# An LSTM over 512 steps with its input projection by fast matrix multiplication: when the bias differences are made, how far ahead sums run, and when finished blocks of the head are stored

## The chip, the core and the metric

The kernel runs on one core of a Trainium2 chip. The core has a matmul engine (TensorE, PE in the profile), three engines for elementwise work (VectorE, DVE; ScalarE, ACT; GpSimd, POOL) and SyncE (SP), which issues all of this kernel's DMAs. Each engine takes its instructions in order, and they wait for one another by semaphores. The metric is the device time of one execution in microseconds (us).

## The reference

`x` has 32 rows of 512 steps with 512 features. An LSTM runs over the steps, started from `cond_1024`, and its outputs are added to `x`:

```python
xW = jnp.einsum('ntd,dg->ntg', x, Wx) + b          # 4*512 gate columns
def step(carry, xw_t):
    prev_h, prev_c = carry
    a = xw_t + prev_h @ Wh
    i, f, o = sigmoid of a's first three quarters
    g = jnp.tanh(a[:, 3 * Hd:])
    next_c = f * prev_c + i * g
    next_h = o * jnp.tanh(next_c)
    return ((next_h, next_c), next_h)
x = x + all next_h
```

All data are float32. The gate bias `b` is drawn with a spread of 0.1, so it is not zero.

## The kernel before

**A step.** Step t needs its row of xW in a PSUM bank. TensorE adds `h @ Wh` to it (`h_part`, L272: 16 matmuls of 128x512, which the profile counts as 32). Then `cell` runs: ScalarE's sigmoids and tanh (L285 to L290, from step 18 on L298 to L305), VectorE's products (L288, L289, L291; later L302 to L307) and a transpose that gives the next `h` (L292, later L309). The next `h_part` needs that `h`. TensorE fills the time in between with the projection `x @ Wx`.

**The projection, from step 19 on.** Steps 19 to 498 form 15 groups of 32 steps. A group's projection is done by a fast matrix multiplication in two levels. The outer level has 26 products ("slots"), each of a sum of x blocks (U, `U_SUMS`, `U_OF`; made on VectorE by `make_sum`, L504, in eight buffers, `free_u`) and a sum of weight blocks (V, `V_SUMS`, `V_OF`), where V is the same in all groups. The inner level does each slot by seven products of half size, `ROW` (L590). Four copies or adds bring a slot's result out of PSUM into one of some 16 buffers (`free_c`; `evacuate`, L656 to L672). Sums of results (W, `W_SUMS`, `W_OF`; `w_op`, L450, 128x1024 on VectorE) give 16 output blocks a group. A finished block is appended to `done_blocks`; `store_blocks` (L463) issues its DMA to DRAM (L467), gives its buffer back to `free_c` and counts it in `gr.stored`. `load_xw` (L723) brings the rows of a step back (L732), and ScalarE puts them into the step's bank (L743).

**The head, steps 0 to 18.** Their projection is done plainly, 32 matmuls of 256 columns a block and step (`plain_block`, L200), while VectorE makes the V sums (`v_sum`, L781 and L784, with `v_store`, L788, into DRAM `vdram`) and the x sums of group 0 (`pair_sum`, L535 to L541, of rows that `load_row`, L525, brings). V sums 8 to 25 live in ten rooms (`V_ROOMS`), which are parts of other buffers, so a room is written again only after the store of what stood in it. `load_v` (L703, L708) brings V rows back for the slots from number 4 on. The rows of steps 5 to 18 start from a copy of the bias into their bank: L960 for step 0's two plain blocks (14 and 15), L1074 for the following steps'. Finished rows of steps 14 to 18 are parked in DRAM (`kept`, L874, loaded again at L726).

**Bias differences.** In the groups, the bias enters through some of the slots' banks, which start from one of six rows: -b2, b0-b3, b3, b0-b1+b2, b1, b1-b0 (`BIAS_OF`, `seed_tile`; ScalarE copies them in, L633). `make_seeds` (L831) computes these rows from `seeds_at`, a tile of 64 partitions with the four bias rows, each as two halves of 4 elements a partition (also subtracting the first half from the second), and stores them in DRAM (L843). `load_seeds` (L845) loads them, spread over all partitions, from step 3 on.

**What sets the order.** The program is one list written out by a planner; every engine follows its part of the list. In the head, each step t emits `h_part`, the stores that wait, and then chunks (`HEAD_PLAINS` plain blocks, `HEAD_STREAM` quarters of products). A stream chunk of m quarters first calls `load_v_ahead`, `store_blocks` and `u_ahead(m)`, which makes every U sum that the next m quarters need, then `evacuate`. A chunk after the cell calls `row_jobs(4)`, `u_ahead(m + 24)` and then `w_op` as long as the planner's account `room["dve"]` allows; then come the matmuls. The cell of a step stands after its first chunk (from step 10 on, after its second). `room["dve"]` is an account in ns: matmuls add to it, every operation on VectorE takes its cost (`cost_dve`: 150 + 1.05 a column, 1225 for a W sum, 1091 for a U sum). `jobs` are the V sums and the like of the first steps, shared out over a step's chunks. From step `HEAD_STEPS` = 19 on, the loop sets the account to `3800 + min(0, room)` at each step and calls `w_op` while it is over 1000; it calls `store_blocks` after every `w_op`.

**SyncE's queue** issues DMAs in the order of the list. There are eight semaphores for them in turn, so each DMA waits until the one eight before it has landed, and a store that waits for VectorE holds up all that is behind it.

Of the kernel before, what the change touches and what calls it, by code (L numbers as in the profile page):

```python
# [7 lines left out]
F32 = mybir.dt.float32  # L8
# [97 lines left out]
def kernel(  # L106
# [59 lines left out]
    def load_x_ahead():  # L166
        nc.sync.dma_start(
            out=xnat[:, 2, 0 : HEAD - 2 * TC].rearrange("p t q b -> p (t q b)"), in_=x[2][:, 0 : (HEAD - 2 * TC) * P]
        )
# [253 lines left out]

    wait_to_store = [True]

    def w_op(short=False):
# [35 lines left out]

    def store_blocks():  # L463
        for gr, o, buf, src in done_blocks:
            mo, j = divmod(o, 4)
            tau = TAU.index(mo)
            nc.sync.dma_start(  # L467
                out=xwd[gr.g % 2][2 * tau : 2 * tau + 2, :, j].rearrange("m p c -> p m c"),
                in_=buf_of(buf).rearrange("p (m n) c -> p m (n c)", m=2),
            )  # L470
            if src is None:
                free_c.append(buf)
            else:
                release(gr, src)
            gr.stored[tau] += 1
        done_blocks.clear()

# [349 lines left out]

    seeds_at = work.tile([P // 2, 10, 2, 4], F32, name="seeds_at")
    by_part = lambda a: a.rearrange("j (h p k) -> p j h k", h=2, p=P // 2)

    def make_seeds():  # L831
        b = [seeds_at[:, i] for i in range(4)]
        neg2, d03, b3, all3, b1, d10 = (seeds_at[:, 4 + i] for i in range(6))
        for j in range(4):
            sub(seeds_at[:, j, 1], seeds_at[:, j, 1], seeds_at[:, j, 0])
        sub(d10, b[1], b[0])
        sub(neg2, b[1], b[2])
        sub(neg2, neg2, b[1])
        sub(d03, b[0], b[3])
        nc.scalar.copy(b3, b[3])  # L840
        nc.scalar.copy(b1, b[1])
        sub(all3, b[2], d10)
        nc.sync.dma_start(out=by_part(seed_dram), in_=seeds_at[:, 4:10])  # L843

# [31 lines left out]
    with tc.manual_schedule():  # L876
        nc.vector.memset(sring[0], 0.0)
        nc.vector.memset(tanh_c, 0.0)
        nc.scalar.activation(hbuf, tanh_c, AF.Sigmoid)
        load_x(0, 0, 5)  # L880
# [11 lines left out]
        for j in range(NJ):  # L892
            nc.sync.dma_start(
                out=bias_full[j * B : (j + 1) * B], in_=bias[j : j + 1].to_broadcast([B, W])
            )
        nc.sync.dma_start(out=seeds_at[:, 0:4], in_=by_part(bias))
        nc.sync.dma_start(out=h_init.rearrange("p q b -> p (q b)"), in_=h0)
# [6 lines left out]
        load_x(1, 0, 5)  # L904
        load_x_ahead()
        for n in range(4):
            for j in range(NJ):
                nc.tensor.matmul(
                    park_banks[n % 3][j * B : (j + 1) * B],
                    tanh_c[:, 0:B],  # L910
                    tanh_c.unsqueeze(1).to_broadcast([P, 4, P]),
                    start=True,
                    stop=True,
                )
# [15 lines left out]
        keep(FIRST)  # L930
        make_seeds()
        jobs = {}
        sums = lambda *ids: [lambda i=i: v_sum(i) for i in ids]
        jobs[0] = sums(13, 14, 15, 16)
        jobs[1] = sums(17, 18, 19, 20)
        jobs[2] = sums(21, 22, 23)
# [25 lines left out]
        for t in range(T):  # L962
# [4 lines left out]
            kept_stores.clear()  # L967
            store_blocks()
            c, rest = divmod(t + 6, TC)
# [25 lines left out]
            if t < HEAD_STEPS:  # L995
# [22 lines left out]
                for i, (kind, m, cs) in enumerate(chunks):  # L1018
# [16 lines left out]
                    else:  # L1035
                        load_v_ahead()
                        store_blocks()
                        u_ahead(m)
# [6 lines left out]
                        else:  # L1045
                            row_jobs(4)
                            u_ahead(m + 24)
                            while wqueue and (
# [35 lines left out]
            if t == HEAD_STEPS:  # L1084
                room["dve"] = max(room["dve"], -2600.0)
            wait_at_end[0] = t >= END - 2
# [86 lines left out]
```

## Time and profile before

| | us |
|---|---|
| median of 3 runs | 3084.79 (3084.72 to 3087.29) |
| profiled execution | 3085.83 |
| its span, first to last instruction | 3084.1 |
| TensorE busy, share of the span | 3061.4, 99% |
| VectorE busy | 2340.9, 76% |
| ScalarE busy | 1466.8, 48% |
| GpSimd busy | 243.0, 8% |
| mean granted TensorE clock | 0.999 |
| moved by DMA | 753.21 MB, mean 244 GB/s |

How to read the lines that follow. A timeline line has start and length in us, engine, line of the kernel, operation, output<-inputs, shapes, count, and in brackets how long the engine had been idle and what released it. SPq marks an issue on SyncE's queue, PEld the load of a matmul's stationary operand. A line of waits has engine, output and line, the instruction waited for, and then the sum in us, how often, and the longest. Where an instruction waited for several, the view names the one that came last by the profile, and this can be another engine than the one that truly held it up.

### The profile page before, as it was taken

To read this page: it belongs to the slowest core of one execution; us is meant where nothing else is said; L and a number is where in the kernel's file an instruction comes from. 1 tells how busy PE (TensorE), PEld (TensorE's weight loads), DVE (VectorE), ACT (ScalarE), POOL (GpSimd) and SP (SyncE) were. 2 spreads that over 40 slices of the span, in tenths; PEclk is the share of its full clock that TensorE was granted. 3 is DMA by queue.
4 is the path that set the end of the run, shared out by engine and by line. 5 is a ranking of instruction groups with operands and counts; after the bars stand their busy time and mean duration, and the time that the engine had idled before them with its cause. 6 is when DMAs were issued, how large, how long until landed. Compare 5 with 4: busy or idle time off the path is not lost.

```text
span 3084.1 us, 108287 instructions
## 1 busy us (share of the span) xinstructions
PE 3061.4 (99%) x43624; PEld 1658.8 (54%) x43624; DVE 2340.9 (76%) x6310; ACT 1466.8 (48%) x5476; POOL 243.0 (8%) x508
## 2 busy tenths in 40 slices
PE   9999999999999999999999999999999999999998
PEld 5755555555555555555555555555555555555675
DVE  7588787787877878778787887878778787787644
ACT  1344545445454544545444444454544545454444
POOL 0000000000000000000000000000000000000110
PEclk9999999999999999999999999999999999999999
DMA  9888878787787878878787787877878777788530
GB/s 319 272 288 279 272 246 262 241 259 243 252 260 243 259 243 257 256 231 274 232 268 243 242 272 234 271 239 243 267 241 260 242 247 263 245 264 270 162 91 18
DMA packets 320149, 753.21 MB, mean 244 GB/s; under 512 B 52128, under 2 KB 103968, under 8 KB 319136
## 3 DMA queue, kind: packets, MB, share of 16 engines
q1 hardware_dynamic: 319648, 746.28, 75.3%
q8 instruction: 344, 5.64, 0.8%
q14 instruction: 157, 1.29, 0.1%
HBM read 564.67 MB, written 184.56 MB: 243 GB/s over the span
## 4 chain that ended last, share of the span: by engine, by line
PE 97%; DVE 1%; DMA 1%; ACT 0%; issue 0%; SPq 0%; ACTq 0%; DVEq 0%
PE gbank L272 54%; PE xbank L590 32%; PE bbank L590 5%; PE xbank L272 3%; PE xbank L209 1%; PE gbank L200 1%; PE xbank L200 1%; DMA r<-in_L_cond_Wx_dram 0%; PE bbank L200 0%; DMA r<-in_x_grouped_dram 0%; DMA vring<-in_L_cond_Wx_dram 0%; DVE cbuf L450 0%; DVE vring L784 0%; DVE ubuf L784 0%; DVE xnat L450 0%
## 5 line engine op out<-in xcount | busy, mean ns | idle before, releaser
L272 PE MATMUL gbank<-wh_sb,ht 128*32 128x512 f32 (+1 forms) x16256 | 1775.3, 575 | 4.0 <-DVE ht L309 1.6
L272 PEld LDWEIGHTS gbank<-wh_sb,ht 128*32 128x32 f32 x16256 | 606.7, 110 | 825.9 <-issue 700.0
L590 PE MATMUL xbank<-vring,ubuf 128*32 128x256 f32 (+1 forms) x13584 | 852.4, 369 | 5.8 <-ACT cbuf L672 2.3
L298 ACT ACTIVATE s<-gbank 128x128 f32<-128x128 f32 x944 | 264.7, 281 | 1162.9 <-PE gbank L272 1162.3
L590 PEld LDWEIGHTS xbank<-vring,ubuf 128*32 128x32 f32 x13584 | 527.7, 110 | 298.4 <-issue 136.0
L302 DVE TENSOR_TENSOR prod<-s 128x128 f32<-128x128 f32 x988 | 283.6, 287 | 461.6 <-ACT s L299 457.0
L317 POOL TENSOR_TENSOR oc<-xnat,ht 128x128 f32<-128x128 f32 x504 | 242.8, 482 | 2803.1 <-DVE ht L309 1294.9
L305 ACT ACTIVATE tanh_c<-s 128x64 f32<-128x64 f32 x988 | 253.6, 257 | 234.6 <-DVE s L303 232.0
L309 DVE STREAM_TRANSPOSE ht<-hbuf 128x64 f32<-128x64 f32 x986 | 242.0, 245 | 72.5 <-DVE hbuf L307 0.9
L743 ACT COPY gbank<-xw 128x512 f32<-128x512 f32 x458 | 275.3, 601 | 2.7 <-DMA xw<-xwd 2.4
L303 DVE TENSOR_TENSOR s<-prod 128x64 f32<-128x64 f32 x988 | 222.2, 225 | 34.0
L307 DVE TENSOR_TENSOR hbuf<-o,tanh_c 128x64 f32<-128x64 f32 x988 | 204.6, 207 | 31.8 <-ACT tanh_c L305 31.2
L450 DVE TENSOR_TENSOR cbuf<-cbuf 128x1024 f32<-128x1024 f32 x178 | 216.6, 1223 | 1.0
L299 ACT ACTIVATE s<-gbank 128x64 f32<-128x64 f32 x944 | 217.0, 230 | 0.0
L590 PE MATMUL xbank<-vring,r 128*32 128x256 f32 (+1 forms) x3216 | 208.6, 357 | 0.0
L590 PE MATMUL xbank<-vring,xs 128*32 128x256 f32 (+1 forms) x3120 | 202.4, 356 | 0.0
L590 PE MATMUL bbank<-vring,ubuf 128*32 128x256 f32 (+1 forms) x2600 | 185.0, 342 | 0.0
L590 PEld LDWEIGHTS xbank<-vring,r 128*32 128x32 f32 x3216 | 123.4, 110 | 78.8 <-issue 46.0
L590 PEld LDWEIGHTS xbank<-vring,xs 128*32 128x32 f32 x3120 | 120.8, 110 | 57.8 <-issue 22.8
L300 ACT ACTIVATE o<-gbank 128x128 f32<-128x128 f32 (+1 forms) x493 | 148.7, 302 | 0.0
L656 ACT COPY cbuf<-xbank 128x512 f32<-128x512 f32 x228 | 132.7, 582 | 27.8 <-PE xbank L590 15.4
L590 PEld LDWEIGHTS bbank<-vring,ubuf 128*32 128x32 f32 x2600 | 101.2, 110 | 67.7 <-issue 38.6
(171 smaller groups left out, 2558.0 us busy)
## 6 DMA issues: line engine op xcount, KB each, us to landing
vring<-vdram SPq DMA_DIRECT2D x310, 896.0 KB, 6.2
xw<-xwd SPq DMA_DIRECT2D x1920, 64.0 KB, 4.6
xwd<-cbuf SPq DMA_DIRECT2D x142, 512.0 KB, 4.7
xwd<-r SPq DMA_DIRECT2D x79, 512.0 KB, 4.4
out_dram<-oc SPq DMA_DIRECT2D x255, 128.0 KB, 3.6
xnat<-in_x_dram SPq DMA_DIRECT2D x62, 512.0 KB, 5.4
xs<-in_x_grouped_dram SPq DMA_DIRECT2D x45, 512.0 KB, 4.7
vring<-vdram SPq DMA_DIRECT2D x33, 512.0 KB, 5.0
```

Source lines behind the costliest of these rows:

```text
L272: nc.tensor.matmul(dst[j * B : (j + 1) * B], state["ht"][:, k], m, start=False, stop=True, skip_group_check=True)
L298: nc.scalar.activation(s[:, u, 0:2], g[:, n_, 0:2], AF.Sigmoid)
L299: nc.scalar.activation(s[:, u, 2], g[:, n_, 3], AF.Tanh)
L302: nc.vector.tensor_mul(prod[:, u], s[:, u, 0:2], s[:, u, 2:4])
L303: add(nxt[:, u, 3], prod[:, u, 0], prod[:, u, 1])
L305: nc.scalar.activation(tanh_c[:, HALVES[u]], nxt[:, u, 3], AF.Tanh)
L307: nc.vector.tensor_mul(hbuf[:, HALVES[u]], o[:, u], tanh_c[:, HALVES[u]])
L309: nc.vector.transpose(ht[:, 2 * u : 2 * u + 2].rearrange("p q b -> p (q b)"), hbuf[:, HALVES[u]])
L317: (nc.gpsimd if t < T - 8 else nc.vector).tensor_add(oc[:, tt % 2], x_of(t), ht)
L450: op(c_of(dst), c_of(src), c_of(bb))
L590: nc.tensor.matmul(dst[j * B : (j + 1) * B, cols], left_of(gr, s, r)[:, j * B : (j + 1) * B], right_of(row, slot, RIGHT[r])[:, cols], star ...
L743: nc.scalar.copy(bank_of(t), src)
```

## The change

Four edits.

1. **Bias differences.** The four bias rows are loaded by four DMAs (one a row) after the head's x loads, in place of one DMA ahead of `h0` and `Wh`. They land where the results want them (b1 and b3 in their final place), -b2 is now zero minus b2 (its row is set to zero at the start), where it was b1 - b2 - b1, and three of the four half differences are one operation. `make_seeds` has six operations on VectorE and none on ScalarE, where it had nine and two, and is called between the V sums 19 and 20 of step 1; before, it was called ahead of step 0. Its store moves along.
2. **Stores.** In steps 0 to 14 `store_blocks` leaves the blocks that were finished since its last call for the next call, if more than three buffers are free.
3. **U sums.** In the last chunk of steps 7 to 16 the look-ahead is `m + 40` quarters in place of `m + 24`, if more than one U buffer is free.
4. **Step 19.** The planner's account is set to -2000 there; before, it was only raised to -2600 where it was below.

```diff
+    old = [0]
...
-    def store_blocks():
-        for gr, o, buf, src in done_blocks:
+    def store_blocks(keep_new=False):
+        fresh = done_blocks[old[0] :] if keep_new and len(free_c) > 3 else []
+        for gr, o, buf, src in done_blocks[: len(done_blocks) - len(fresh)]:
...
-        done_blocks.clear()
+        done_blocks[:] = fresh
+        old[0] = len(fresh)
...
-    seeds_at = work.tile([P // 2, 10, 2, 4], F32, name="seeds_at")
+    seeds_at = work.tile([P // 2, 8, 2, 4], F32, name="seeds_at")
...
+    BIAS_AT = (6, 4, 7, 2)
+
     def make_seeds():
-        b = [seeds_at[:, i] for i in range(4)]
-        neg2, d03, b3, all3, b1, d10 = (seeds_at[:, 4 + i] for i in range(6))
-        for j in range(4):
-            sub(seeds_at[:, j, 1], seeds_at[:, j, 1], seeds_at[:, j, 0])
-        sub(d10, b[1], b[0])
-        sub(neg2, b[1], b[2])
-        sub(neg2, neg2, b[1])
-        sub(d03, b[0], b[3])
-        nc.scalar.copy(b3, b[3])
-        nc.scalar.copy(b1, b[1])
-        sub(all3, b[2], d10)
-        nc.sync.dma_start(out=by_part(seed_dram), in_=seeds_at[:, 4:10])
+        neg2, d03, b3, all3, b1, d10, b0, b2 = (seeds_at[:, i] for i in range(8))
+        sub(seeds_at[:, 2:8:2, 1], seeds_at[:, 2:8:2, 1], seeds_at[:, 2:8:2, 0])
+        sub(b2[:, 1], b2[:, 1], b2[:, 0])
+        sub(d10, b1, b0)
+        sub(neg2, neg2, b2)
+        sub(d03, b0, b3)
+        sub(all3, b2, d10)
+        nc.sync.dma_start(out=by_part(seed_dram), in_=seeds_at[:, 0:6])
...
         nc.vector.memset(tanh_c, 0.0)
+        nc.vector.memset(seeds_at[:, 0], 0.0)
...
-        nc.sync.dma_start(out=seeds_at[:, 0:4], in_=by_part(bias))
         nc.sync.dma_start(out=h_init.rearrange("p q b -> p (q b)"), in_=h0)
...
         load_x_ahead()
+        for j in range(NJ):
+            nc.sync.dma_start(out=seeds_at[:, BIAS_AT[j] : BIAS_AT[j] + 1], in_=by_part(bias[j : j + 1]))
...
         keep(FIRST)
-        make_seeds()
...
-        jobs[1] = sums(17, 18, 19, 20)
+        jobs[1] = sums(17, 18, 19) + [make_seeds] + sums(20)
...
-            store_blocks()
+            store_blocks(t < HEAD - 4)
...
-                        store_blocks()
+                        store_blocks(t < HEAD - 4)
...
-                            u_ahead(m + 24)
+                            u_ahead(m + (40 if i == len(chunks) - 1 and 6 < t < HEAD_STEPS - 2 and len(free_u) > 1 else 24))
...
             if t == HEAD_STEPS:
-                room["dve"] = max(room["dve"], -2600.0)
+                room["dve"] = -2000.0
```

## The prediction, made before the changed kernel ran

> **What bounds the kernel now.** I read the page first, then TensorE's own waits, then the timeline of each engine in the first 310 us, then the DMA share in windows there.
>
> ```profile
> PE 3061.4 (99%) x43624; PEld 1658.8 (54%) x43624; DVE 2340.9 (76%) x6310; ACT 1466.8 (48%) x5476; POOL 243.0 (8%) x508
> PE 97%; DVE 1%; DMA 1%; ACT 0%; issue 0%; SPq 0%; ACTq 0%; DVEq 0%
> ```
>
> TensorE is busy for all but 22.7 us of the 3084.1 us span, and it is 97% of the chain that ended last. The change adds and removes no matmul, so all that it can win is TensorE's idle time, plus time at a lowered clock. TensorE's waits, longest first:
>
> ```profile
> PE xbank L200 <- ACT xbank L960: 4.1, 1, 4.1
> ...
> PE xbank L590 <- ACT cbuf L672: 2.3, 2, 1.5
> PE xbank L590 <- ACT xbank L633: 1.7, 1, 1.7
> ...
> PE gbank L272 <- DMA wh_sb<-in_L_cond_Wh_dram: 1.3, 1, 1.3
> PE gbank L272 <- DVE hbuf L307: 1.1, 1, 1.1
> PE xbank L590 <- ACT xnat L672: 0.9, 1, 0.9
> ```
>
> All of these stand in steps 0 to 19. Asked for 240 us onward, the same view holds the L307 wait alone (it begins at 239.0), until the last steps' waits for h at L309. What can be won therefore lies in the first 240 us.
>
> **The seeds (make_seeds and its loads).** The largest wait, on TensorE and on ScalarE:
>
> ```profile
> 31.89 1.06 PE L272 MATMUL gbank<-wh_sb,ht 128*32 128x512 f32 x8 [1.35 <-DMA wh_sb<-in_L_cond_Wh_dram]
> 37.07 6.11 PE L200 MATMUL xbank<-r,xnat 128*32 128x256 f32 x64 [4.11 <-ACT xbank L960]
> ```
>
> ```profile
> 36.24 0.20 ACT L840 COPY seeds_at<-seeds_at 64x8 f32<-64x8 f32 x1 [33.90 <-DVE seeds_at L835]
> ```
>
> ```profile
> 16.00:20.00 4.00, 4.00 (x82) 3.26 (x75) 1.68 (x3) 0.00 (x0) 0.00 (x0) 1.00 0.46 89
> 37.00:42.00 5.00, 4.93 (x48) 2.54 (x49) 3.45 (x7) 1.48 (x6) 1.08 (x1) 0.50 0.74 248
> 54.00:56.00 2.00, 2.00 (x44) 1.59 (x40) 2.00 (x4) 0.24 (x1) 0.00 (x0) 1.00 0.32 121
> ...
> 83.00:89.00 6.00, 6.00 (x87) 3.90 (x81) 5.18 (x8) 1.80 (x5) 1.21 (x1) 1.00 0.19 69
> 175.00:200.00 25.00, 23.27 (x340) 12.03 (x336) 18.42 (x34) 9.69 (x26) 1.67 (x2) 1.00 0.81 286
> ```
>
> (Windows: stretch, length, then busy us of PE, PEld, DVE, ACT, POOL, the granted clock, DMA share, GB/s.) The copy at L960 puts the bias under step 0's plain blocks. It needs only bias_full, but on ScalarE's in-order queue it stands behind L840, which waits 33.9 us for VectorE to reach make_seeds. The change takes both small copies off ScalarE, so L960 can run as soon as the bias is loaded, and the 4.11 us go. The stall also halved the granted clock (0.50 from 37 to 42 us): 4.93 us of work at half speed is 2.46 us lost. The gap of 1.7 us in step 13 leaves the clock at 1.00 (175 to 200), so this goes too.
>
> SyncE's queue there:
>
> ```profile
> 11.26 0.64 SPq L896 DMA_DIRECT2D seeds_at<-in_L_cond_b_dram  x1
> 14.65 0.35 SPq L897 DMA_DIRECT2D ht<-in_cond_dram  x1
> 18.34 2.05 SPq L899 DMA_DIRECT2D wh_sb<-in_L_cond_Wh_dram  x4
> ```
>
> These issues come one by one, each when an earlier transfer has landed (eight semaphores in rotation). Without L896 the h0 load takes its turn at 11.26 and the first wh row the turn at 14.65, 3.7 us sooner, into a stretch where the DMA share is 0.46 (0.54 x 4 = 2.2 us unused). wh is what TensorE awaits for 1.35 us at 31.89. Bounds 0 and 1.35; I take 1.35, since 2.2 us exceed it. The four bias loads now stand behind the x loads, and behind them on SyncE the first V stores, whose rooms are not written again before step 2. VectorE reads the biases some 20 us later, so I take 0; uncovered, four issues like L896's are 2.6 us of SyncE. The added memset falls before VectorE's first sum, while it waits for weights. **Offered to TensorE: 4.11 + 2.46 + 1.35 = 7.9 us.**
>
> How much survives? VectorE must now keep up, and its queue is nearly full here:
>
> ```profile
> 35.84 0.36 DVE L835 TENSOR_TENSOR seeds_at<-seeds_at 64x4 f32<-64x4 f32 x4
> ...
> 38.04 0.43 DVE L288 TENSOR_TENSOR prod<-s 128x256 f32<-128x256 f32 x1 [1.34 <-ACT s L286]
> ...
> 39.56 0.31 DVE L292 STREAM_TRANSPOSE ht<-hbuf 128x128 f32<-128x128 f32 x1
> ...
> 47.12 1.28 DVE L784 TENSOR_TENSOR ubuf<-cbuf 128x768 f32<-128x768 f32 x2
> 50.72 0.43 DVE L288 TENSOR_TENSOR prod<-s 128x256 f32<-128x256 f32 x1 [2.32 <-ACT s L286]
> ...
> 59.65 1.28 DVE L784 TENSOR_TENSOR xs<-cbuf,vring 128x768 f32<-128x768 f32 x2
> 61.06 0.43 DVE L288 TENSOR_TENSOR prod<-s 128x256 f32<-128x256 f32 x1
> ...
> 73.42 0.99 DVE L535 TENSOR_TENSOR xs<-xs 128x512 f32<-128x512 f32 x1
> ...
> 77.12 1.29 DVE L784 TENSOR_TENSOR vring<-cbuf,ubuf 128x768 f32<-128x768 f32 x2
> 81.74 0.43 DVE L288 TENSOR_TENSOR prod<-s 128x256 f32<-128x256 f32 x1 [3.33 <-ACT s L286]
> ...
> 83.35 0.31 DVE L292 STREAM_TRANSPOSE ht<-hbuf 128x128 f32<-128x128 f32 x1
> ```
>
> Step 0's cell (L288 to the end of L292, 1.83 us) can start when make_seeds used to, at about 35.9: h at 37.8. The V sums of step 0 (to 48.40) then end at 46.3, where cell 1 follows without its old 2.32 us of idling: h at 48.1. Step 1's sums (8.4 us, from cell 1's end at 52.55 to 60.93) and the six seed operations (four took 0.36 us; I take 0.6) end at 57.1, cell 2's h at 59.0. TensorE wants it at 67.09 - 7.9 = 59.2 (the third h product started at 67.09):
>
> ```profile
> 67.09 3.69 PE L272 MATMUL xbank<-wh_sb,ht 128*32 128x512 f32 x32
> ...
> 84.32 3.69 PE L272 MATMUL gbank<-wh_sb,ht 128*32 128x512 f32 x32
> ```
>
> So far nothing is handed back, with 0.2 us to spare: what VectorE takes beyond that, TensorE loses. What is late next are the x rows that step 3's sums (L535) read:
>
> ```profile
> L525 SPq DMA_DIRECT2D xs<-in_x_grouped_dram x2: 522/760/997, 65.5 to 66.5; - x2
> ...
> DMA to landing us min/median/max: 6.0/6.4/6.8
> ```
>
> The second lands at 66.5 + 6.8 = 73.3, just as L535 starts. DMA is full around it, so the rows come earlier only by what the queue gains: 2.1 us because the first V sums end 2.1 us earlier, and 0.68 x 2 = 1.4 us from the hole at 54 to 56. Against that stands the seed store, moved from a hole into this full stretch:
>
> ```profile
> 39.00:43.00 4.00, 4.00 (x52) 2.12 (x46) 3.73 (x7) 0.20 (x1) 1.08 (x1) 0.63 0.45 129
> ```
>
> It is 768 pieces of 16 bytes, and in the window where it ran the engines were busy for 0.45 x 4 = 1.8 us in all. Bounds 0 and 1.8; I take 0.7, since ordinary stores shared that window. The rows then land 3.5 - 0.7 = 2.8 us sooner (1.7 to 3.5), at 70.5. From landing to the last sum take 5.1 us (73.3 to 78.4), the cell 1.9 us (81.74 to 83.66): h at 77.5 where TensorE took it at 84.32 without waiting. **What survives: 6.7 us, bounds 5.5 and 7.9.** Behind step 4 the steps wait on TensorE in turn and DMA has nothing queued until the next sum is done, so the shift is kept.
>
> The Trainium skill (DMA: Bandwidth & Descriptors, Specifications and Measured) speaks against this store: it says that an engine does a read-modify-write below 512 B, and that small packets cost about 10.5 ns each. That makes 8.1 us for 768, an estimate; the rows would land 4.6 us late and the sum would be 3084.3. The window above, with under 2 us of busy engines, disagrees.
>
> **Step 19.** Ahead of the wait at L307:
>
> ```profile
> 237.31 1.22 DVE L450 TENSOR_TENSOR xnat<-cbuf,xnat 128x1024 f32<-128x1024 f32 x1
> 238.45 0.28 DVE L302 TENSOR_TENSOR prod<-s 128x128 f32<-128x128 f32 x1
> ...
> 303.18 0.29 DVE L302 TENSOR_TENSOR prod<-s 128x128 f32<-128x128 f32 x1 [2.17 <-ACT s L299]
> ```
>
> The planner's own costs (1225 for a W sum), added up along steps 0 to 18, leave -654, so step 19 may spend 3146: two sums of 1225 above the limit of 1000. From -2000 it has 1800: one. The sum at 237.31 goes, the cell starts 1.14 us sooner, and **1.1 us** of wait end. The sum runs later: by its counts the planner has used up its queue by step 30, where VectorE idles 2.17 us ahead of the cell, more than the 1.22 us; uncovered, it would give the 1.1 us back.
>
> **U sums farther ahead.** Three waits above are really for a U sum, which ends after the ScalarE copy that the view names:
>
> ```profile
> 183.57 1.09 DVE L504 TENSOR_TENSOR ubuf<-xs,ubuf 128x896 f32<-128x896 f32 x1
> ```
>
> TensorE resumes 0.1 us after it (the L633 wait). But the new reach falls short of it. Counted in quarters of a product, row k starts at 48 + 28(k-3). Step 12's last chunk starts at 408 and reaches 408 + 52 - 1 = 459; this sum is for slot 18, at 468. Step 14's reaches 579, slot 22 starts at 580; step 15's reaches 635, slot 24 starts at 636. Only the sums of slots 13 and 15 move up, each changing places with one W sum ahead of the same cell. I take 0; the bounds are a loss of 0.15 (a W sum's 1.22 for a U sum's 1.07 ahead of a cell) and a gain of the three waits, 1.7 + 1.5 (the longer of the two at cbuf L672) + 0.9 = 4.1 us.
>
> **Stores one chunk later** (steps below 15, more than three buffers free). This lets loads pass SyncE's wait for a sum. But no wait in TensorE's list is for a V row, so 0; a gain is bounded by the waits just named, a loss is rival 4.
>
> **Sum:** 6.7 + 1.1 = 7.8 us off the span: 3076.3. The profiled execution took 3085.83 with a span of 3084.1; the median of the runs is 3084.79. Off the median: **3077.0 us**.
>
> **The rivals.**
> 1. *The x rows are late.* The store costs its 1.8 us, and the loads, 512 pieces, 1.2 more: the rows land 0.5 us sooner, 4.5 us survive, with step 19 5.6: 3079.2. For it: the queue is full around the rows. Against: the loads come before the hole at 39 to 43 us, which can take them in.
> 2. *The seed store holds up the full queue for as long as it took to land.* The DMA view has that as its last number (us):
>
> ```profile
> seed_dram<-seeds_at SPq DMA_DIRECT2D x1, 12.0 KB, 5.9
> ```
>
>    The rows would land 5.9 - 3.5 = 2.4 us late, at 75.7, h at 82.7; 1.6 us survive, with step 19 2.7: 3082.1. For it: 16-byte pieces. Against: landing includes waiting behind other stores, and the window's 1.8 us.
> 3. *The U sums do arrive.* 7.8 + 4.1 = 11.9: 3072.9. Against: the counts above, which miss by one quarter twice.
> 4. *Slower: buffers come free in another order.* Holding blocks back in steps 11 to 14 changes the order of the free list, which all 15 groups inherit. If in each one an evacuation copy finds its buffer's store still under way and TensorE loses 1.5 us, that is 22.5 us: 3099.5. From 0.52 us per group (7.8/15) on, the kernel is slower. Against: no such wait reaches TensorE after 240 us now.
> 5. *The copies at L960 stay late* for another reason, so the change does not do what it says there: step 19 alone, 3083.7. Against: they read nothing but the bias.
>
> **How the numbers follow.** Forecast 0.60 (own range 3075.6 to 3078.6), rivals in order 0.20, 0.03, 0.06, 0.07, 0.04. A measurement of this kernel tells 0.2% (6.2 us, a time below 3078.6) from no change. Faster takes nearly all of the forecast, rival 3 and a quarter of rival 1, whose prices are upper ends: 0.67. Within 0.2% lie the rest of rival 1, rivals 2 and 5 and the edge of the forecast: 0.26. Slower 0.07. The range leaves out rivals 3, 4 and 5, which is 0.17: 3074.0 to 3082.5.
>
> **What would show it.** Right: L960 ends before 30 us, the clock is 1.00 from 37 to 42 us, no L200 wait; the h product of step 5 starts near 77.6; the wait before step 20's h product is gone; the waits at L590 in steps 13, 15 and 16 stay. Wrong in size: L535 starts later than 71. Wrong in kind: TensorE waits after 250 us, or ScalarE waits for a store in every group.

## The result, and the profile after

The changed kernel takes 3080.61 us in the median of 21 executions (3079.64 to 3083.92), against 3084.79 of the kernel before, also of 21 (3083.63 to 3090.39): ratio 0.9986, 95% interval 0.9980 to 0.9992. It is faster by 4.2 us, where 7.8 had been forecast. The profiled execution took 3080.49 us with a span of 3078.7, so the spans differ by 5.4 us. The profiled execution of before had been 1.0 us above its median, this one is 0.1 below; that alone makes the 5.4 a 4.2.

The page's line of engines and the chain:

```profile
PE 3059.3 (99%) x43624; PEld 1652.5 (54%) x43624; DVE 2338.9 (76%) x6308; ACT 1466.5 (48%) x5474; POOL 242.9 (8%) x508
PE 97%; DVE 2%; DMA 1%; ACT 0%; issue 0%; SPq 0%; DVEq 0%; ACTq 0%
```

TensorE still does the same matmuls; it idles for 19.4 us in place of 22.7, and the other 2.1 us of the 5.4 are busy time, mostly what the stretch at half clock had added. (Lines of the changed kernel stand two or three higher: L450 is now L451, L504 L507, L590 L593, L633 L636, L656 L659, L672 L675.) TensorE's waits of the changed kernel:

```profile
PE xbank L593 <- ACT cbuf L675: 2.2, 2, 1.5
PE gbank L272 <- ACT tanh_c L305: 2.0, 1, 2.0
...
PE xbank L593 <- ACT xbank L636: 1.7, 1, 1.7
...
PE xbank L272 <- DVE ht L292: 1.0, 1, 1.0
PE xbank L593 <- ACT xnat L675: 0.9, 1, 0.9
```

The waits of 4.1 (L200), 1.3 (Wh) and 1.1 us (L307) are gone. Three U-sum waits (1.5, 1.7, 0.9) are as they were. Two waits are new: 1.0 us for an `h` of the head (L292), and 2.0 us that the view puts down to a tanh. The view counts idle time from a modelled end of the matmuls ahead, so what a wait costs can be more than its entry: the table that follows goes from start to start, and there the new wait of 1.0 us costs 1.25 at the h product of step 3 (8.13 us sooner at step 2, 6.88 at step 3).

Where the time came from can be followed by the start of the h products, which stand in the same order in both kernels. In the table, each row gives by how much the h product of that step starts sooner than in the profiled execution of before:

| h product of step | starts before | after: sooner by | what happened on the way |
|---|---|---|---|
| 1 | 46.41 | 8.15 | bias copies early, no half clock, Wh early (7.9 forecast) |
| 3 | 67.09 | 6.88 | the new wait of 1.0 us |
| 5 | 84.32 | 6.58 | x rows late by 0.3 (6.7 forecast) |
| 12 | 164.00 | 7.46 | a wait for a V row in step 11 gone |
| 20 | 240.09 | 8.73 | step 19's wait gone (1.1 forecast) |
| 23 | 257.73 | 6.52 | the new wait of 2.0 us in step 22 |
| 35 | 328.53 | 6.45 | |
| 499 | 3021.95 | 6.13 | small losses, see the last section |

Two more small losses behind step 499 make the 5.4 us of the span.

ScalarE and TensorE in the first steps, from the timeline of the changed kernel, and the clock in the window that had been at half:

```profile
20.38 0.59 ACT L962 COPY xbank<-bias_full 128x512 f32<-128x512 f32 x1 [18.04 <-DMA bias_full<-in_L_cond_b_dram]
20.90 0.58 ACT L962 COPY bbank<-bias_full 128x512 f32<-128x512 f32 x1
31.58 0.38 ACT L285 ACTIVATE s<-gbank 128x256 f32<-128x256 f32 x1 [10.09 <-PE gbank L272]
```

```profile
27.85 3.69 PE L272 MATMUL gbank<-wh_sb,ht 128*32 128x512 f32 x32
31.28 1.09 PE L200 MATMUL xbank<-r,xnat 128*32 128x256 f32 x15
```

```profile
37.00:42.00 5.00, 5.00 (x68) 2.09 (x64) 4.53 (x8) 2.41 (x6) 1.08 (x1) 1.00 0.70 261
```

The bias copies (L960, now L962) wait for the bias alone and are done at 21.5, where they had ended at 37.5. Step 0's h product runs without a break, the plain block follows at once, and the granted clock is 1.00 where it had been 0.50.

VectorE and TensorE around the seeds and the x rows:

```profile
54.71 0.15 DVE L838 TENSOR_TENSOR seeds_at<-seeds_at 64x12 f32<-64x12 f32 x1
...
55.14 0.15 DVE L843 TENSOR_TENSOR seeds_at<-seeds_at 64x8 f32<-64x8 f32 x1
56.16 0.96 DVE L787 TENSOR_TENSOR xs<-r,vring 128x768 f32<-128x768 f32 x1 [0.87 <-DMA vdram<-xs]
...
58.24 0.42 DVE L288 TENSOR_TENSOR prod<-s 128x256 f32<-128x256 f32 x1
...
71.15 0.69 DVE L538 TENSOR_TENSOR xs<-xs 128x512 f32<-128x512 f32 x1 [2.72 <-DMA xs<-in_x_grouped_dram]
...
75.76 0.42 DVE L288 TENSOR_TENSOR prod<-s 128x256 f32<-128x256 f32 x1
```

Here the new wait of 1.0 us is born. Behind the six seed operations VectorE waits 0.87 us to write V sum 20 into a room in `xs`, until the V sum that stood there has been stored; step 2's cell begins at 58.24 in place of some 57.1, and its `h` is late. The seed operations (0.6 us) stand inside this wait: without them VectorE would only have waited longer. Further down, the x rows come at 71.15, and step 4's cell at 75.76.

Step 22, the 2.0 us. First the changed kernel (VectorE, SyncE, ScalarE, TensorE), then what ScalarE's copy found in the kernel before:

```profile
228.59 1.22 DVE L451 TENSOR_TENSOR cbuf<-cbuf,xnat 128x1024 f32<-128x1024 f32 x1
229.72 0.29 DVE L302 TENSOR_TENSOR prod<-s 128x128 f32<-128x128 f32 x1
...
233.49 1.22 DVE L451 TENSOR_TENSOR xnat<-cbuf,xnat 128x1024 f32<-128x1024 f32 x1
```

```profile
242.57 0.39 SPq L469 DMA_DIRECT2D xwd<-xnat  x1
```

```profile
242.56 0.35 ACT L675 COPY r<-xbank 128x256 f32<-128x256 f32 x1
245.86 0.59 ACT L659 COPY xnat<-xbank 128x512 f32<-128x512 f32 x1 [2.94 <-DMA xwd<-xnat]
```

```profile
251.21 1.06 PE L272 MATMUL gbank<-wh_sb,ht 128*32 128x512 f32 x8 [2.00 <-ACT tanh_c L305]
```

```profile
241.70 0.38 SPq L467 DMA_DIRECT2D xwd<-xnat  x1
```

```profile
251.29 0.36 ACT L672 COPY r<-xbank 128x256 f32<-128x256 f32 x1
251.54 0.59 ACT L656 COPY xnat<-xbank 128x512 f32<-128x512 f32 x1
```

The sum that step 19 no longer does finishes output block 6, in the `xnat` buffer. It now runs in step 20 (233.49). Its store is issued at 242.57, because on SyncE's queue it now stands behind step 19's V loads and step 20's xw loads. ScalarE's evacuation of step 22 takes this very buffer and waits for the store to land, and step 22's cell (its sigmoids and its tanh) stands behind that copy on ScalarE. In the kernel before, the store was issued at 241.70 and the copy came at 251.54, ten microseconds later.

### The profile page after: what moved, and what is told of

Same layout as the page of the kernel before. It is cut to its first block, busy times and chain, and to the rows that moved or that the text cites. A ratio compares the mean times of both kernels' runs of the same rounds, so it can differ in the third digit from the quotient of the medians.

```text
span 3078.7 us, 108289 instructions
## 1 busy us (share of the span) xinstructions
PE 3059.3 (99%) x43624; PEld 1652.5 (54%) x43624; DVE 2338.9 (76%) x6308; ACT 1466.5 (48%) x5474; POOL 242.9 (8%) x508
## 4 chain that ended last, share of the span: by engine, by line
PE 97%; DVE 2%; DMA 1%; ACT 0%; issue 0%; SPq 0%; DVEq 0%; ACTq 0%
PE gbank L272 54%; PE xbank L593 33%; PE bbank L593 5%; PE xbank L272 3%; PE xbank L209 1%; PE gbank L200 1%; DMA r<-in_L_cond_Wx_dram 0%; DVE xs L787 0%; DVE ubuf L787 0%; DVE vring L787 0%; DMA vdram<-xs 0%; DVE prod L302 0%; PE bbank L200 0%; PE xbank L200 0%; DVE s L303 0%
## 5 line engine op out<-in xcount | busy, mean ns | idle before, releaser
L593 PE MATMUL xbank<-vring,ubuf 128*32 128x256 f32 (+1 forms) x13584 | 852.3, 369 | 5.4 <-ACT cbuf L675 2.2
L593 PEld LDWEIGHTS xbank<-vring,ubuf 128*32 128x32 f32 x13584 | 528.2, 110 | 297.4 <-issue 135.6
L307 DVE TENSOR_TENSOR hbuf<-o,tanh_c 128x64 f32<-128x64 f32 x988 | 204.3, 207 | 31.7 <-ACT tanh_c L305 31.4
L451 DVE TENSOR_TENSOR cbuf<-cbuf 128x1024 f32<-128x1024 f32 x178 | 216.4, 1222 | 0.9
L593 PE MATMUL xbank<-vring,r 128*32 128x256 f32 (+1 forms) x3216 | 208.5, 357 | 0.0
L593 PE MATMUL xbank<-vring,xs 128*32 128x256 f32 (+1 forms) x3120 | 202.5, 356 | 0.0
L593 PE MATMUL bbank<-vring,ubuf 128*32 128x256 f32 (+1 forms) x2600 | 184.9, 342 | 0.0
L593 PEld LDWEIGHTS xbank<-vring,r 128*32 128x32 f32 x3216 | 123.2, 110 | 78.9 <-issue 46.3
L593 PEld LDWEIGHTS xbank<-vring,xs 128*32 128x32 f32 x3120 | 120.8, 110 | 57.8 <-issue 22.9
L659 ACT COPY cbuf<-xbank 128x512 f32<-128x512 f32 x228 | 132.6, 582 | 28.4 <-PE xbank L593 17.4
L593 PEld LDWEIGHTS bbank<-vring,ubuf 128*32 128x32 f32 x2600 | 101.1, 110 | 67.6 <-issue 38.7
```

The costliest lines, as they stand in the source:

```text
L307: nc.vector.tensor_mul(hbuf[:, HALVES[u]], o[:, u], tanh_c[:, HALVES[u]])
L451: op(c_of(dst), c_of(src), c_of(bb))
L593: nc.tensor.matmul(dst[j * B : (j + 1) * B, cols], left_of(gr, s, r)[:, j * B : (j + 1) * B], right_of(row, slot, RIGHT[r])[:, cols], star ...
```

## The experiments

All times are medians against the kernel before, run on the same chip between them; its medians there were 3084.9 to 3085.9. "Sooner" is as in the table above, from the profiled execution of each run.

| run | what it is | median, us | ratio, 95% interval | sooner at steps 5, 12, 20, 23, 499 |
|---|---|---|---|---|
| e1_seeds | edit 1 alone | 3080.05 | 0.9984 (0.9975 to 0.9994) | 6.89, 7.62, 7.65, 7.64, 5.83 |
| e2_stores | edit 2 alone | 3085.86 | 1.0000 (0.9991 to 1.0010) | 0.95, 0.87, 0.87, 0.87, 0.87 |
| e3_usums | edit 3 alone | 3086.77 | 1.0001 (0.9992 to 1.0010) | -0.73, -0.75, -0.75, -0.75, -1.25 |
| e4_step19 | edit 4 alone | 3088.98 | 1.0012 (1.0003 to 1.0021) | -0.77, -1.43, -0.17, -2.28, -5.06 |
| f1_split_load | before, bias load in four | 3085.21 | 0.9998 (0.9988 to 1.0008) | 0.80, 0.42, 0.43, 0.43, 0.44 |
| f2_finish_first | after, other sum in step 19 | 3083.60 | 0.9994 (0.9985 to 1.0003) | 7.41, 7.53, 4.98, 3.56, 2.83 |
| f3_reach_52 | f2 with reach m + 52 | 3076.92 | 0.9970 (0.9959 to 0.9982) | 7.44, 8.02, 13.70, 8.59, 8.56 |
| f4_store_after_x | after, seed store later | 3081.93 | 0.9989 (0.9979 to 0.9999) | 7.49, 8.35, 9.63, 7.22, 5.13 |
| g1_reach_52_only | edit 1 and reach m + 52 | 3074.07 | 0.9967 (0.9954 to 0.9979) | 7.11, 8.56, 13.43, 13.43, 12.10 |
| g2_copies_moved | before, two copies moved | 3082.15 | 0.9992 (0.9983 to 1.0001) | 6.46, 6.18, 6.19, 6.19, 3.74 |
| g3_four_stores | after, seed store four times | 3089.71 | 1.0014 (1.0004 to 1.0024) | 3.48, 2.40, 3.66, 0.31, -0.06 |
| h1_other_phase | g1, 17 tiny operations more | 3075.12 | 0.9963 (0.9950 to 0.9977) | 6.98, 8.27, 12.17, 12.17, 11.11 |

**Each edit alone.** The four edits of the diff above, one at a time, on the kernel before.

Edit 1:

> The bias edit alone on the kernel before. Theory: it makes all of the head's gain. The h product of step 1 starts about 8.1 us sooner than before, step 2 likewise, step 3 6.9 and step 5 6.6 us sooner, and 6.6 us are still there at step 10; the wait before step 20's h product (1.1 us) stays, no wait of 2 us follows in step 22: span 3084.1 - 6.6 = 3077.5, or 3076.6 if the 0.86 us that step 11 gained in the changed kernel come from this edit too (its rotation of semaphores on SyncE differs by three). Rival A: step 22's stall comes from the new order in the head, then the span is 3079.7. Rival B: part of the 6.6 us needs the other edits: step 10 less than 6 us sooner.

Step 5 is 6.89 us sooner, step 20 7.65, and nothing happens in step 22: the bias edit makes the head's gain by itself, and rivals A and B fall. Its ratio, 0.9984, is that of the whole change (0.9986): taken together, the other three edits add nothing. The span came to 3078.2 and not to 3076.6, because 1.8 us were lost between steps 23 and 499.

Edit 2:

> The held-back stores alone on the kernel before. Theory: the 0.86 us of step 11 come from here, since the V loads no longer stand behind a store that waited 4.5 us for VectorE; nothing else changes: span 3083.2. Rival A (the 0.86 us are the bias edit's): 3084.1, with the 0.39 us wait of step 11 in place. Rival B: the other order of buffers costs a wait in the groups, or the stall of step 22 (2 us): 3086 or more.

The 0.9 us sooner are there from step 1 on, so they are another start of the head. Step 11 has its wait still, and here the view names what it is for:

```profile
PE xbank L593 <- DMA vring<-vdram: 0.8, 1, 0.8
```

In the kernel before, where the view names VectorE's L666, this row landed at 156.96 us, just as L666 ended, and TensorE went on at 157.09. In f1_split_load, below, TensorE went on before L666 had ended. So the V row was the reason in the kernel before too. The stores gained nothing and cost nothing. The theory about step 11 fell.

Edit 3:

> The longer look-ahead alone on the kernel before. Theory: no wait goes, since the reach ends one quarter short; the three waits of 1.67, 1.45 and 0.87 us in steps 13, 15 and 16 stay: span 3084.1 within 0.2. Rival: moving the sums of steps 11 and 12 up takes the 0.86 us out of step 11 (a shorter VectorE queue ahead of its add): 3083.2.

The waits of 1.68, 1.45 and 0.86 us stand, and no step between 1 and 23 changes by more than 0.05: nothing, as expected.

Edit 4:

> The budget of step 19 alone on the kernel before. Theory: the wait of 1.1 us before step 20's h product goes (step 20 1.2 us sooner), and the block whose sum moved to step 20 is stored later, so the ScalarE copy that takes its buffer in step 22 waits for that store and step 23 is 2.2 us later: 1 us slower in all, span 3085.1. Rival: the stall of step 22 needs the other edits; then 1.2 us stay: 3082.9.

Step 20 gains 1.26 us (from -1.43 to -0.17) and step 23 gives back 2.11. ScalarE and TensorE in this run:

```profile
254.66 0.59 ACT L656 COPY xnat<-xbank 128x512 f32<-128x512 f32 x1 [2.84 <-DMA xwd<-xnat]
```

```profile
260.01 1.49 PE L272 MATMUL gbank<-wh_sb,ht 128*32 128x512 f32 x12 [1.90 <-ACT cbuf L672]
```

It is the same copy and the same store as in the changed kernel, with none of the other edits. Edit 4 alone makes the kernel slower. The profiled execution, which took 3091.04 us, is 5.1 us later than before's at step 499; 0.85 of them are this, the rest are another start of the head (0.8), a wait in step 10 (0.7), a V row in step 34 (1.5) and small losses in the groups. The edit changes nothing ahead of step 19, so step 10 is not its work. There a ScalarE copy (L656, at 148.86) found its buffer's store under way: it began 0.1 us after the store had landed, and TensorE waited 0.64 us for it. In the kernel before, the same copy waited for the same store, but that landed 5.7 us after its issue, in place of 8.1 here, and TensorE lost nothing. The view of ScalarE's waits has it:

```profile
ACT cbuf L656 <- DMA xwd<-cbuf: 6.5, 1, 6.5
```

So this kind of stall stood in the profile of before already. Whether the wait in step 34 belongs to the edit was not tried.

**Why step 11 gained.** In front of the loads:

```diff
-        nc.sync.dma_start(out=seeds_at[:, 0:4], in_=by_part(bias))
+        for j in range(NJ):
+            nc.sync.dma_start(out=seeds_at[:, j : j + 1], in_=by_part(bias[j : j + 1]))
```

> The kernel before with its one bias load split into four at the same place, so that the order in which DMAs share SyncE's eight semaphores shifts by three for all that follows, and nothing else changes. Theory: that rotation made the 0.86 us of step 11 in the changed kernel; then steps 10 to 12 here show no wait of TensorE for a V row (their length 0.4 to 0.9 us shorter than before), while the start of the head is up to 2 us worse for three more issues ahead of Wh. Rival: the 0.86 us come from elsewhere in the bias edit (its loads or its store moved); then a wait of 0.4 to 0.9 us stands in steps 10 to 12 as in the kernels with the other single edits.

Between steps 5 and 12 the run loses 0.38 us, and a wait of 0.57 us for a V row stands in step 11. The rotation is not the reason. (The start of the head, up to 2 us worse by the theory, was 0.8 us sooner.) Over all runs, those with the bias edit gain 0.1 to 0.9 us between steps 10 and 12 against the kernel before, and those without it (g2 among them) lose 0 to 0.7 (the 0.7 are e4's copy of step 10). With the edit, the row that step 11 waits for landed 12.8 to 13.8 us behind step 10's h product, without it 13.7 to 14.2; what in that edit does it stays open.

**Step 19 with the other sum.** On the changed kernel, in `w_op`:

```diff
+        if at_19[0]:
+            first = next((q for q in wqueue if q[1] == ("out", 6)), first)
         wqueue.remove(first)
...
+            at_19[0] = t == HEAD_STEPS
             while wqueue and room["dve"] > (1000 if t < END else 2600):
```

> The changed kernel, but step 19's one sum is the one that finishes output block 6, and the sum for block 5 goes to step 20. Theory: block 6 is stored in step 19 again, ahead of the V loads of SyncE's queue, so no ScalarE copy of step 22 meets a store under way: the stall of 2.0 us ahead of the h product of step 22's successor goes, step 20 stays 1.2 us sooner, span 3078.7 - 2.2 = 3076.5. Rival: the copy of step 22 meets another buffer whose store is late, and the stall stays: 3078.7.

Worse than the changed kernel: step 20 gives back 2.56 us, and step 21 1.4 more. The stall of step 22 is gone, as the theory had it, but another takes its place. SyncE and VectorE:

```profile
228.62 0.38 SPq L472 DMA_DIRECT2D xwd<-cbuf  x1
```

```profile
232.34 1.23 DVE L454 TENSOR_TENSOR cbuf<-cbuf,xnat 128x1024 f32<-128x1024 f32 x1 [3.74 <-DMA xwd<-cbuf]
```

Made first, this sum can't be written over one of its operands and takes a free buffer. The free list has only the one whose store (block 7) had been issued 3.7 us earlier, and the sum waits for it with `h` behind. TensorE waits 3.65 us for that, and its granted clock is 0.50 for 3.4 us after (234.56 to 237.98), which is where the 1.4 us of step 21 go. It is the mechanism of step 22 again, one engine over: with one or two free buffers, whoever takes one soon after its store waits for the landing.

**A longer reach.** On f2:

```diff
-u_ahead(m + (40 if i == len(chunks) - 1 and 6 < t < HEAD_STEPS - 2 ...
+u_ahead(m + (52 if i == len(chunks) - 1 and 6 < t < HEAD_STEPS - 2 ...
```

> As the last one, and the look-ahead in the last chunk is m + 52 quarters in place of m + 40, so that the sums for slots 18, 22, 23, 24 and 25 are made a chunk or more sooner. Theory: the three waits of 1.68, 1.45 and 0.87 us in steps 13, 15 and 16 go: 3076.5 - 4.0 = 3072.5. Rival: VectorE, which now has up to two U sums (2.2 us) more ahead of a cell, hands part back as h that comes late, or output blocks finished later put stalls into steps 16 to 30: 3074.5 or more.

The waits for U sums go: between steps 12 and 17 the run gains 4.86 us. Then steps 22 and 23 give back 5.1: a wait of 3.1 us, and half clock for 3.4 us behind it (242.74 to 246.16). TensorE's waits, and ScalarE:

```profile
PE gbank L272 <- DVE hbuf L307: 3.4, 2, 3.1
```

```profile
235.71 0.59 ACT L662 COPY cbuf<-xbank 128x512 f32<-128x512 f32 x1 [3.73 <-DMA xwd<-cbuf]
```

Both theories hold in part: the reach pays all that was asked of it, and output blocks finished later (here two U sums of group 1 had been pulled ahead of them in step 16) put the same kind of stall behind.

**The reach without the stall.** On the kernel before, with edit 1 and:

```diff
-                            u_ahead(m + 24)
+                            u_ahead(m + (52 if i == len(chunks) - 1 and t in (6, 12, 13, 14, 15) else 24))
```

> The kernel before with the bias edit and, in the last chunk of steps 6 and 12 to 15 alone, a look-ahead of m + 52 quarters; the stores and step 19's budget are those of before, so every output block of group 0 is stored in the same step as before. Theory: the bias edit gives its 6.6 us; the waits for U sums 18, 16, 22, 23 and 25 (0.80 in step 7, 1.68, 0.05, 1.45 and 0.87 us in steps 13 to 16) go; the 1.1 us ahead of step 20 stay and no stall follows in steps 20 to 23: 3084.1 - 6.6 - 4.8 = 3072.7, 8 us under the changed kernel's less what its own step 19 nets. Rival: VectorE, given two U sums ahead of one cell, makes h late, or a ScalarE copy meets a store under way: 3075 or more.

Median 3074.07, span 3071.9. TensorE's waits are now, all behind step 1:

```profile
PE xbank L272 <- DVE ht L309: 2.3, 3, 0.8
...
PE gbank L272 <- DVE ht L309: 1.6, 2, 0.8
PE gbank L272 <- DVE hbuf L307: 1.1, 1, 1.1
PE xbank L272 <- DVE ht L292: 0.8, 1, 0.8
PE xbank L590 <- ACT xnat L656: 0.6, 1, 0.6
```

All waits for the U sums named are gone, the 1.1 us of step 19 stay, and steps 20 to 23 lose nothing. This version beats both kernels: 0.9967 of the kernel before, where the change gave 0.9986.

**What the copies alone are worth.** On the kernel before:

```diff
-        nc.scalar.copy(b3, b[3])
-        nc.scalar.copy(b1, b[1])
+        nc.vector.tensor_copy(out=b3, in_=b[3])
+        nc.vector.tensor_copy(out=b1, in_=b[1])
```

> The kernel before with nothing but make_seeds' two copies moved from ScalarE to VectorE; loads, their places and the call stay. Theory: these two copies on ScalarE were the cause of the 4.11 us, and of the halved clock behind them; both go (6.6 us), the wait of 1.35 us for Wh stays, VectorE takes 0.2 to 0.3 us more ahead of cell 0: the h product of step 1 starts 6.3 us sooner than before, and about 6.0 us reach step 5: span 3078.1. Rival: VectorE, with make_seeds still ahead of cell 0, makes h of step 0 the new bound, and less than 4 us reach step 1: 3080 or more.

Step 1 is 6.98 us sooner and step 5 6.46, a little over what the theory gave. The start of the head differs by up to 0.9 us between executions anyway (e2, e3 and e4, which don't touch it, have 0.9, -0.7 and -0.8 at step 1), so the agreement is no closer than that. VectorE:

```profile
36.22 0.16 DVE L840 COPY seeds_at<-seeds_at 64x8 f32<-64x8 f32 x1
...
36.44 0.41 DVE L288 TENSOR_TENSOR prod<-s 128x256 f32<-128x256 f32 x1
...
56.56 0.96 DVE L784 TENSOR_TENSOR xs<-r,vring 128x768 f32<-128x768 f32 x1 [1.73 <-DMA vdram<-xs]
```

Two copies of 0.2 us on another queue make nine tenths of what all of edit 1 makes at step 5 (6.46 of 6.9). And with no seed operation in step 1, VectorE waits 1.73 us ahead of V sum 20 in place of the 0.87 above: the room's store sets its time, the seeds cost nothing there. The median is 2.8 us under before and not 6, because 2.4 us go again between steps 23 and 499, and because the profiled execution of before, from which "sooner" is counted, lay 0.9 us above its median. The interval, 0.9983 to 1.0001, just touches 1.

**What the seed store costs the full queue.** First by moving it, on the changed kernel:

```diff
                 load_row(0, 0)
                 load_row(0, 1)
+                nc.sync.dma_start(out=by_part(seed_dram), in_=seeds_at[:, 0:6])
```

> The changed kernel with the bias rows' store issued behind the two x-row loads of step 2 in place of between V sums 19 and 20. Theory: the store costs the full queue about 0.7 us of transfer, so L535's group, which started at 71.15, starts at 70.5; the time gains at most 0.3 us, since step 5 is now only 0.27 us behind step 4. Rival A: it costs 1.8 us, and the group starts at 69.4. Rival B: it costs next to nothing in the queue, and the group starts at 71.0 to 71.3.

```profile
69.60 0.69 DVE L538 TENSOR_TENSOR xs<-xs 128x512 f32<-128x512 f32 x1 [1.80 <-DMA xs<-in_x_grouped_dram]
```

This can't be read: with the store at its place, the same rows landed between 69.5 and 71.1 in the profiled executions of six kernels (after, e1, f2, f3, g1, h1), so 69.60 is no evidence of anything. Then by issuing it four times, a larger dose:

```diff
-        nc.sync.dma_start(out=by_part(seed_dram), in_=seeds_at[:, 0:6])
+        for k in range(4):
+            nc.sync.dma_start(out=by_part(seed_dram[6 * k : 6 * k + 6]), in_=seeds_at[:, 0:6])
```

> The changed kernel with its bias store issued four times in a row, each to its own rows, of which the last three are never read. With one store the first sum of x rows (L538's group) started at 71.15 in the changed kernel, and the rows landed between 69.5 and 71.1 in four executions of this code. Theory: each store costs the full queue 0.7 us, so three more make it 71.6 to 73.2. Rival A: 1.8 us each: 74.9 to 76.5. Rival B: next to nothing: not later than 71.3. Rival C: 5.9 us each, as long as one took to land: 87 or later.

```profile
74.26 0.69 DVE L538 TENSOR_TENSOR xs<-xs 128x512 f32<-128x512 f32 x1 [6.87 <-DMA xs<-in_x_grouped_dram]
```

Three more stores made the rows 3.1 us later than the changed kernel's 71.15, and at most 4.8 later than the earliest landing of 69.5: 1.0 to 1.6 us each, in one execution. That lies between the theory's 0.7 and rival A's 1.8, and far below rival C. But the trace shows little of it as transfer in the full queue. SyncE took 4.62 us to issue the four stores, where it had taken 1.56 us for the one, so the loads of the x rows behind them were issued at 66.26 in place of 63.35, 2.9 us later. From its issue the first row then took 6.7 us to land, where it had taken 6.3. So nearly the whole delay is the issuing. What one store costs as transfer was not measured: 0.4 us for three is less than landing times differ. And the issuing of one such store took 0.62 to 0.64 us at other places, in the kernel before and in f4; why it takes more here was not tried. (The wait of TensorE that comes of it, 4.03 us ahead of step 5, is followed by 3.4 us at a clock of 0.50, so step 10 is only 1.79 us sooner.)

**The small losses in the groups.** On g1:

```diff
+        for _ in range(9):
+            nc.scalar.copy(hbuf[:, 0:8], tanh_c[:, 0:8])
...
-        nc.vector.memset(seeds_at[:, 0], 0.0)
...
+        for _ in range(9):
+            nc.vector.memset(seeds_at[:, 0], 0.0)
```

> The last kernel but two (bias edit and reach 52), with 8 more tiny memsets on VectorE and 9 more tiny copies on ScalarE in the first 12 us, while both engines idle. What it tests: in the runs so far, each loss of 0.1 to 0.34 us between steps 24 and 499 stood at an instruction whose number on its engine, counted from the start of the trace, is 63 modulo 128, and only where this was the first transpose of a step (VectorE, up to 0.33) or the first tanh of a step (ScalarE, 0.25). Theory: the loss belongs to the number, so the padding moves it to other instructions: of the 4 and 4 such places 1 and 1 are left, the losses at steps 154, 191, 447 and 487 go, and of the 1.4 us lost between steps 99 and 499 at most 0.6 remain: span 3071.9 - 0.9 = 3071.0. Rival: they are chance, or bound to the step: the losses at steps 191 and 447, which four kernels share, stay, span 3071.9 within 0.3.

VectorE in step 153's cell, in g1 and in h1, and then where h1 has its loss:

```profile
1015.37 0.23 DVE L307 TENSOR_TENSOR hbuf<-o,tanh_c 128x64 f32<-128x64 f32 x1
1016.07 0.24 DVE L309 STREAM_TRANSPOSE ht<-hbuf 128x64 f32<-128x64 f32 x1 [0.47 <-DVE hbuf L307]
```

```profile
1017.18 0.23 DVE L307 TENSOR_TENSOR hbuf<-o,tanh_c 128x64 f32<-128x64 f32 x1
1017.51 0.24 DVE L309 STREAM_TRANSPOSE ht<-hbuf 128x64 f32<-128x64 f32 x1
...
1871.28 0.23 DVE L307 TENSOR_TENSOR hbuf<-o,tanh_c 128x64 f32<-128x64 f32 x1
1871.98 0.25 DVE L309 STREAM_TRANSPOSE ht<-hbuf 128x64 f32<-128x64 f32 x1 [0.47 <-DVE hbuf L307]
```

The transpose follows the product by 0.33 us, and by 0.70 where its number on VectorE is 63 modulo 128 (2239 at 1016.07, 4287 at 1871.98). The losses that g1 had at steps 145, 154, 191, 427, 447, 475 and 487 are gone; h1 has 0.13 at step 299 and 0.25 and 0.24 at 464 and 474. Between steps 35 and 499 it loses 0.4 us where g1 lost 1.3: the losses go with the number, as the theory had it. The time isn't better for it (span 3073.3): in this execution the sums of step 19 waited for x rows, 0.88 us of idling on VectorE, which cost 0.95 us at step 20, and 0.7 more went at step 33, where ScalarE waited for a row of xW: transfers, whose landing differs from execution to execution.

## Why the prediction was right, and where it was not

*The copies at L960* (4.11 and 2.46 us): right, both in kind and in size. g2 shows them alone, 6.98 at step 1 against 6.57, within the 0.9 us by which the start of the head differs between executions. *Wh* (1.35 us): it brings the rest; 8.15 in all at step 1, 7.9 forecast.

*How much survives* (6.7, bounds 5.5 to 7.9): 6.58, and 6.89 in e1, so the size is right, but one step of the way to it failed: "Step 1's sums ... and the six seed operations ... end at 57.1, cell 2's h at 59.0", in time for TensorE. I had VectorE's queue without the rooms. V sum 20 must wait until the store of what stood in its room has landed; this made `h` 1.0 us late in the profiled execution and 0 to 1.0 in others. The x rows that I had as the next limit (70.5, `h` at 77.5) came at 71.15, and step 5's h product started at 77.74. Since step 2 had given back 1.0 us already, they took only 0.3 more.

*The seed store* (0.7, bounds 0 and 1.8): 1.0 to 1.6 us by g3, inside the bounds, but of another kind. I had priced the transfer in the full queue; in g3, 2.9 of the 3.1 us came from the time that SyncE took to issue the stores, which is in no term of the sum. The estimate of 8.1 us for its 768 pieces, worked out from the Trainium skill (DMA: Bandwidth & Descriptors, Specifications and Measured), does not agree with g3; the page measured its 10.5 ns on loads that GpSimd issues, and this is a store that SyncE issues. Rivals 1 and 2, which have 4.5 and 1.6 us survive, fall with the 6.58.

*Step 19* (1.1 us): the gain is there, 1.26. The step that failed is its cover: "VectorE idles 2.17 us ahead of the cell, more than the 1.22 us". I asked whether VectorE has time for the moved sum, and it has. But the sum also finishes a block; the block's store moved with it, behind other DMAs on SyncE's queue, and the copy that takes the block's buffer waited for it: 2.2 us, twice the gain. My bound for the uncovered case, 1.1 us, was too small as well. It is the mechanism of rival 4, an evacuation copy that finds its buffer's store still under way. I had given it to the held-back stores and to all 15 groups; it came from step 19's edit and once. e4 shows it alone. A wait of this kind, 6.5 us on ScalarE in step 10, stood in the profile of before (shown under e4), and I had passed over it, because it reached no wait of TensorE.

*U sums* (0, since the reach falls one quarter short): right, by e3; and g1 shows that 12 quarters more take those waits away, so rival 3 was a question of reach only. *Stores* (0): right, by e2. But "no wait in TensorE's list is for a V row" was wrong: the 0.4 us in step 11 were one, under VectorE's name.

*Not in the sum at all:* the 0.9 us of step 11, which the bias edit brought by a way that stays open, and 1.1 us of small losses behind step 23, which the last section explains in part.

From 7.8 to 5.4 by step: seeds 6.58 for 6.7, step 11 +0.9, step 19 1.27 for 1.1, step 22 -2.2, the rest -1.1. The measured 4.2 has in it that I took the whole difference off the median of before, though its profiled execution lay 1.0 us above it.

The time fell into the range, but in part by luck. 3080.61 lies outside the forecast's own 3075.6 to 3078.6; it lies inside the stated range because that had room for rivals 1 and 2 (3079.2 and 3082.1), and neither of them is what happened. Two of the signs of being wrong that I had named did appear: the group of L535 (now L538) began at 71.15, later than 71, and TensorE waits after 250 us, at 251.21.

## What to carry to other kernels

Before an operation is called covered because its engine idles later, follow its output: who stores it, behind what on that queue, and who takes the buffer next; with one or two free buffers a store that takes 3 to 4 us to land decides. A tiny operation with a late input costs what stands behind it on its in-order queue, here two copies of 0.2 us some 6 us. And a look-ahead that misses by one unit does nothing, so count its reach against the place where it is needed.

## What the runs showed of the hardware that I had not expected

On VectorE and ScalarE an instruction can start late when its number on its engine, counted from 0 at the start of the trace, is 63 modulo 128. A step's first transpose (VectorE) then starts 0.68 to 0.70 us behind its product in place of 0.33: in the 14 profiled executions of this case, between 320 and 2850 us, the 41 first transposes with such a number came late, and no other transpose did. On ScalarE it is not as regular: of the 27 first tanhs of a step with such a number, 14 came after 0.50 us of idling in place of 0.22, and the other 13 were not late. TensorE lost up to 0.34 us by one of the transposes, and 0.25 by some of the tanhs. So adding or removing an instruction anywhere ahead moves these losses through the whole program: between steps 35 and 499, against the kernel before, they come to 2.5 us in g2, 1.3 in e1 and g1, 0.4 in h1 and none in e2. The Trainium skill (Runtime: NRT & Kernel Launch, Instruction fetch mechanics) says that instructions are fetched in blocks of 256 and that the cost of crossing one is mostly hidden; the rows have something at every 128, with a price. That it is the fetch was not tried.

Landing times of one and the same code differed by up to 1.6 us between executions where the DMA queue is full (the x rows of step 2: 69.5 to 71.1). Up to 0.7 us of that stood already in the issue of their loads (62.65 to 63.35).

A long wait of TensorE was followed by a granted clock of 0.50: for 3.4 us after waits of 3.1 (f3), 3.65 (f2) and 4.0 us (g3), and again for 3.4 us after the 4.3 us of e2, but for 6.8 us after the 4.1 us of the kernel before. After waits of 2.0 to 2.2 us (after, f4, h1) the clock stayed at 1.00, and so it did after another one of 3.1 us (step 23 of g3). So near 3 us the length of the wait does not settle it; what else does was not tried.
